# Seven-stage attention with VectorE's and ScalarE's instructions held in written order

## The chip, the cores and the metric

The kernel runs on one core of a Trainium2 chip. The metric is the device time of one execution in microseconds; the median of three runs before the change is 8564.84 us (8560.8, 8564.84 and 8583.75). A core has five engines with an instruction stream each: PE (TensorE, matrix products; PEld is its loading of weights), DVE (VectorE), ACT (ScalarE), POOL (GpSimd, here it only starts gathers) and SP (SyncE, here it starts loads and stores). They work side by side and wait for each other through semaphores.

## The reference, cut to what matters

A graph of 12500 nodes with 256 features and 200000 edges, sorted by their target node. Three neighbourhood-averaging layers come first, then an attention step over the same edges. The change touches the attention alone:

```python
x = _layernorm(x + sage(x))                          # three layers, not touched
ZU = einsum('nd,kdr->knr', Z, U)                     # 4 heads of 16
zs, zd = ZU[:, src, :], ZU[:, dst, :]
logits = (zs * zd).sum(-1) / 4
alpha = softmax of logits over the edges of one dst
agg = segment_sum(alpha[..., None] * zs, dst)        # per head and node
ssa = einsum('k,knr,kdr->nd', softmax(head_w), agg, U)
Z_half = 0.5 * Z + 0.5 * ssa
DZ = Z_half @ Dmat.T
grad_step = Z_half + 0.5 * ((Z_half - DZ @ Dmat) @ Dmat)
x = _layernorm(x + relu(grad_step - 0.05))
```

## The kernel before, in words

`fast_sage` computes the three layers, and `fast_attention` the rest. In the profiled execution attention starts at about 6106 us and runs to the end.

Attention cuts the sorted edges into 112 groups of 14 x 128 edges. A group's edges end in a window of 128 target nodes; a node whose edges run over a border is carried into the next group. For each group:

- SP loads the window's rows: `zn` (64 projected features of the targets), `zb` (the features to which the step is added), `zT` (the features turned, for the gradient), and into `ohT` the edges' target positions, spread over 128 partitions.
- POOL gathers the 14 x 128 source rows of 64 features into `zs`, 14 indirect DMAs (line 119). There are six `zs` buffers, so the gathers of group g can start only when group g-6 has read its own for the last time, in `wf` (L1002).
- DVE makes the one-hot matrix `oh` (L453) and ACT its transpose `ohT` (Abs L974, Relu L975). ACT and DVE split `zn` into a rounded part and a rest, `z2` (L979, L980).
- PE multiplies `ohT` by `z2`, 14 products in two halves (`pD`, L986): each edge's target row. There are two `pD` buffers in PSUM, one for each half.
- For each half, DVE multiplies `zs` by `pD` (`zz`, L993) and sums (`lg`, L996), ACT takes the exponential (L999) and copies it to PSUM (`pe`, L1001), DVE weights `zs` (`wf`, L1002), and ACT and DVE split it into `w` (L1005, L1006).
- PE sums `w` over the edges of each node: 14 products of `oh` and `w` and one that carries the last group's rest (`pA`, L1009, L460, with `sh` made by DVE at L459). ACT and DVE add the two parts (`part` L1016, `acc` L1018), DVE divides (`den` L384, L385, `ag` L387), PE turns the result (`pT`, L1022), ACT copies it (`agT`, L394).
- PE makes the gradient step, two products of `zT` (L376) and one of `agT` (L377) into `pO`; ACT applies the relu (L401), DVE adds `zb` (L402) and normalizes (L332, L333, sqrt on ACT L335, L336, L337); SP stores (L435).

`pA`, `pT` and `pO` have one PSUM buffer each. The exponential and the square root need different function tables on ACT, so a table load stands ahead of each once a round.

A group is a generator of five parts, and a round of the loop runs the first part of a new group and then the next part of each of the four groups before it. PE's products are chained in the order in which the program writes them (`in_order`). DVE's and ACT's instructions are not: the scheduler of the build orders them. In the built program one round's order is, on PE: pT, pA with its carry, pD, L376, L377. On ACT: z2, Exp of the first half, relu, pe, Exp, pe, w, Abs, w, sqrt, agT, Relu, part. On DVE: both wf, den's reciprocal, the addition of zb, wlo, ag, the norm's statistics, z2's rest, wlo, the norm, the one-hot, zz, acc, lg, zz, den, sh, lg.

Two helpers are needed to read the diff. `after(first, then)` holds two instructions of one engine in that order, without a semaphore. `store_rows` puts the store on SP behind the instruction that made the tile.

Of the kernel before, what the change touches and what calls it, by code (L numbers as in the profile page):

```python
# [22 lines left out]
P = 128  # L23
# [24 lines left out]
def tile_gnn_resnorm(  # L48
# [137 lines left out]
    with tc.tile_pool(name="prep", bufs=1) as prep, \  # L186
# [136 lines left out]
        nc.vector.tensor_mul(hrow, hrow, hrec)  # L323
        nc.vector.tensor_scalar(gu, ptu[:KR, :], hrow, 0.5, op0=OP.mult, op1=OP.mult)


    def layernorm(wk, y, o):

        n = y.shape[0]
        st = wk.tile([n, nc.vector.BN_STATS_DIM], F32, name="bn_st")  # L330
        mv = wk.tile([n, nc.vector.BN_AGGR_DIM], F32, name="bn_mv")
        nc.vector.bn_stats(st, y)  # L332
        nc.vector.bn_aggr(mv, st)  # L333
        rs = wk.tile([n, 1], F32, name="bn_rs")
        nc.scalar.activation(rs, mv[:, 1:2], AF.Sqrt, bias=eps_t[:n])  # L335
        nc.vector.reciprocal(rs, rs)  # L336
        return nc.vector.tensor_scalar(o, y, mv[:, 0:1], rs, op0=OP.subtract, op1=OP.mult)  # L337

    def sage_end(wk, l, wts, po, hn, xb):

# [36 lines left out]
        mm.append(nc.tensor.matmul(pg, agT, gu, start=False, stop=True))  # L377
        return pg, mm[0], mm[-1]

    def attention_mean(wk, acc, eps, op):  # L380

        n = acc.shape[0]
        den = wk.tile([n, K], F32, name="den")
        nc.vector.tensor_scalar(den, acc[:, KR:AW], eps, None, op0=op)  # L384
        nc.vector.reciprocal(den, den)  # L385
        ag = wk.tile([n, KR], F32, name="ag")
        nc.vector.tensor_mul(ag.rearrange("p (k r) -> p k r", r=R),  # L387
                             acc[:, :KR].rearrange("p (k r) -> p k r", r=R),
                             den.unsqueeze(2).to_broadcast([n, K, R]))
        return ag  # L390

    def attention_turned(wk, pt, n):
        agT = wk.tile([KR, n], F32, name="agT")
        nc.scalar.activation(agT, pt[:KR], AF.Copy)  # L394
        return agT

    def attention_end(wk, zz, pg):

        n = zz.shape[0]
        g = wk.tile([n, D], F32, name="g")  # L400
        nc.scalar.activation(g, pg, AF.Relu, bias=shrink[:n])  # L401
        nc.vector.tensor_add(g, zz, g)  # L402
        return g, layernorm(wk, g, g)

# [40 lines left out]
        nc.vector.tensor_copy(c, iota[:, :n])  # L447
        return c

    def onehot(wk, nodes, r, dt=F32, name="oh", op=OP.is_equal, bufs=2):  # L450

        oh = wk.tile([P, GT, P], dt, name=name, bufs=bufs)
        nc.vector.tensor_tensor(oh, r.unsqueeze(2).to_broadcast([P, GT, P]),  # L453
                                nodes.unsqueeze(1).to_broadcast([P, GT, P]), op=op)
        return oh

    def carry(wk, pa, d, before):
        sh = wk.tile([P, P], F32, name="sh")
        nc.vector.tensor_scalar(sh, steps, d, None, op0=OP.is_equal)  # L459
        return nc.tensor.matmul(pa, sh, before, start=False, stop=True)  # L460

    def fast_sage():
# [482 lines left out]
    def fast_attention():  # L945
        loads[0] = None
        H = GT // 2
        with tc.tile_pool(name="att", bufs=2) as wk, \
                tc.tile_pool(name="att_c", bufs=1, space=PSUM) as cps, \
                tc.tile_pool(name="att_ps", bufs=1, space=PSUM) as ps:  # L950
            nodes = group_consts(cps)
            order, sums = [None], [None]

            def in_order(first, last):
                if order[0] is not None:
# [3 lines left out]
            def group(g):  # L959

                zb = wk.tile([P, D], F32, name="zb", bufs=8)
                zT = wk.tile([P, DC, P], F32, name="zT", bufs=6)
                zn = wk.tile([P, KR], F32, name="zn", bufs=3)
                load_rows([(zn, zu_d), (zb, z_d), (zT, zt_d)], g)

                ohT = wk.tile([P, GT, P], F32R, name="ohT", bufs=3)
                rT = ohT.bitcast(F32).rearrange("p j e -> p (j e)")
                nc.sync.dma_start(rT, rel_d[g * GT:(g + 1) * GT, :].rearrange("j e -> (j e)")[None, :]
                                  .to_broadcast([P, GT * P]))
                zs = wk.tile([P, GT, KR], F32, name="zs", bufs=6)  # L970
                for j in range(GT):
                    gather(zs[:, j], zu_d, srcI[:, g, j:j + 1])
                oh = onehot(wk, nodes, rel[:, g], F32R, bufs=3)
                nc.scalar.activation(ohT.rearrange("p j e -> p (j e)"), rT, AF.Abs, bias=npidx)  # L974
                nc.scalar.activation(ohT.rearrange("p j e -> p (j e)"), rT, AF.Relu, scale=-1.0, bias=1.0)  # L975

                z2 = wk.tile([P, K, 2, R], F32R, name="z2", bufs=3)
                zk = zn.rearrange("p (k r) -> p k r", r=R)
                nc.scalar.activation(z2[:, :, 0], zk, AF.Copy)  # L979
                nc.vector.tensor_tensor(z2[:, :, 1], zk, z2.bitcast(F32)[:, :, 0], op=OP.subtract)  # L980

                w = wk.tile([P, GT, 2 * AW], F32R, name="w", bufs=3)
                for a in (0, H):

                    pd = ps.tile([P, (H + 1) * 2 * KR], F32, name="pD", bufs=2)
                    mm = [nc.tensor.matmul(pd[:, j * 2 * KR:(j + 1) * 2 * KR], ohT[:, a + j],  # L986
                                           z2.rearrange("p k i r -> p (k i r)"), start=True, stop=True)
                          for j in range(H)]
                    in_order(mm[0], mm[-1])

                    zg = zs[:, a:a + H].rearrange("p t (k r) -> p (t k) r", r=R)
                    zz = wk.tile([P, H * K, 2, R], F32, name="zz")
                    nc.vector.tensor_mul(zz, zg.unsqueeze(2).to_broadcast([P, H * K, 2, R]),  # L993
                                         pd[:, :H * 2 * KR].rearrange("p (m i r) -> p m i r", i=2, r=R))
                    lg = wk.tile([P, H, K], F32, name="lg")
                    nc.vector.reduce_sum(lg.rearrange("p t k -> p (t k)"), zz.rearrange("p m i r -> p m (i r)"),  # L996
                                         axis=AX.X)
                    wf = wk.tile([P, H, AW], F32, name="wf")
                    nc.scalar.activation(wf[:, :, KR:], lg, AF.Exp, scale=0.25)  # L999
                    pe = pd[:, H * 2 * KR:H * (2 * KR + K)].rearrange("p (t k) -> p t k", k=K)  # L1000
                    nc.scalar.activation(pe, wf[:, :, KR:], AF.Copy)  # L1001
                    nc.vector.tensor_mul(wf[:, :, :KR].rearrange("p t (k r) -> p t k r", r=R),  # L1002
                                         zs[:, a:a + H].rearrange("p t (k r) -> p t k r", r=R),
                                         pe.unsqueeze(3).to_broadcast([P, H, K, R]))
                    nc.scalar.activation(w[:, a:a + H, :AW], wf, AF.Copy)  # L1005
                    nc.vector.tensor_tensor(w[:, a:a + H, AW:], wf, w.bitcast(F32)[:, a:a + H, :AW], op=OP.subtract)  # L1006
                yield
                pa = ps.tile([P, 2 * AW], F32, name="pA")
                mm = [nc.tensor.matmul(pa, oh[:, j], w[:, j], start=j == 0, stop=g == 0 and j == GT - 1)  # L1009
                      for j in range(GT)]  # L1010
                if g:
                    mm.append(carry(wk, pa[:, :AW], delta[:, g:g + 1], sums[0]))
                in_order(mm[0], mm[-1])
                yield
                part = wk.tile([P, AW], F32, name="part")
                nc.scalar.activation(part, pa[:, AW:2 * AW], AF.Copy)  # L1016
                acc = wk.tile([P, AW], F32, name="acc", bufs=3)
                nc.vector.tensor_add(acc, part, pa[:, :AW])  # L1018
                sums[0] = acc
                ag = attention_mean(wk, acc, 1e-30, OP.max)  # L1020
                pt = ps.tile([P, P], F32, name="pT")
                mm = nc.tensor.transpose(pt[:KR], ag, ident)  # L1022
                in_order(mm, mm)
                yield
                agT = attention_turned(wk, pt, P)
                pg, *mm = gradient_step(ps, zT, agT)
                in_order(*mm)
                yield
                o, made = attention_end(wk, zb, pg)
                store_rows([(o, out)], g, made)  # L1030
                yield

            live = []
            for g in range(NG + 4):
                if g < NG:
                    live.append(group(g))
                    next(live[-1])
                old = live[:-1] if g < NG else live  # L1040
                for s in old:
                    next(s)
                if g >= 4:
                    live.pop(0)
            assert not live


    NTE = E // TE
# [104 lines left out]
    def general_attention():  # L1153
# [40 lines left out]
        with tc.tile_pool(name="go", bufs=1) as wk, tc.tile_pool(name="go_ps", bufs=1, space=PSUM) as ps:  # L1194
            with tc.For_i(0, NBLK, 1) as i:
# [7 lines left out]
                pt = ps.tile([P, NB], F32, name="pT")  # L1203
                nc.tensor.transpose(pt[:KR], attention_mean(wk, ab, 1e-16, OP.add), ident[:NB, :NB])
                pg = gradient_step(ps, zT, attention_turned(wk, pt, NB))[0]
                o, _ = attention_end(wk, zb, pg)
                nc.sync.dma_start(out[rows, :], o)

    ok = nc.values_load(flag[0:1, 0:1], min_val=0, max_val=1)
# [40 lines left out]
```

## Time and profile before

| | us |
|---|---|
| median of three runs | 8564.84 |
| profiled execution, its own time | 8592.77 |
| its span | 8591.0 |
| busy PE, PEld | 5679.5, 4428.1 |
| busy DVE | 3946.6 |
| busy ACT | 3631.0 |
| busy POOL | 4832.6 |
| attention's first gather starts | 6106.16 |
| the last round of gathers starts | 8482.39 |

Busy time is the time in which an engine worked on its own instructions; it covers the whole kernel. POOL's records are the issuing of the gathers. Since the stages have different limits, the sums over the whole span say little about attention, which is the last 29% of it. Durations of single instructions in a steady round of attention, in us: gather 0.94 (0.30 from one to the next), zz 1.08, lg 1.08, one-hot 2.02, wf 0.62, wlo 0.65, Abs 1.77, Relu 1.68, w copy 0.60, table load 1.28, relu 0.47, the norm's statistics 0.42 and its last step 0.41, addition of zb 0.39; 14 pD or 14 pA products 3.23 each. All times are from one profiled execution. The end of a matrix product in the records is worked out by the profiler, not observed; a wait that is put down to "issue" or "remote" is one for which the profile shows no releaser.

### The profile page before, as it was taken

To read this page: it belongs to the slowest core of one execution; us is meant where nothing else is said; L and a number is where in the kernel's file an instruction comes from. 1 tells how busy PE (TensorE), PEld (TensorE's weight loads), DVE (VectorE), ACT (ScalarE), POOL (GpSimd) and SP (SyncE) were. 2 spreads that over 40 slices of the span, in tenths; PEclk is the share of its full clock that TensorE was granted. 3 is DMA by queue.
4 is the path that set the end of the run, shared out by engine and by line. 5 is a ranking of instruction groups with operands and counts; after the bars stand their busy time and mean duration, and the time that the engine had idled before them with its cause. 6 is when DMAs were issued, how large, how long until landed. Compare 5 with 4: busy or idle time off the path is not lost.

```text
span 8591.0 us, 86683 instructions
## 1 busy us (share of the span) xinstructions
PE 5679.5 (66%) x23308; PEld 4428.1 (52%) x23308; DVE 3946.6 (46%) x10013; ACT 3631.0 (42%) x6727; POOL 4832.6 (56%) x5038
## 2 busy tenths in 40 slices
PE   4677777777768888887578878888334444444445
PEld 3455455556646666666466666666233333333334
DVE  4555444433433344444344545454344544444445
ACT  2444444444434444444344444444234444344444
POOL 5555555555555555555455555555456665666663
PEclk8788888888878888998789989998655555555555
DMA  7645555567656666666466666666222222223222
GB/s 208 223 159 166 164 166 183 189 210 228 213 160 199 196 211 208 212 208 200 143 187 193 196 192 205 193 198 182 77 75 85 84 84 83 83 84 86 84 83 69
DMA packets 878810, 1367.37 MB, mean 159 GB/s; under 512 B 191090, under 2 KB 533130, under 8 KB 874207
## 3 DMA queue, kind: packets, MB, share of 16 engines
q1 hardware_dynamic: 629744, 802.71, 28.9%
q0 software_dynamic: 216000, 504.16, 20.9%
q10 hardware_dynamic: 32559, 54.81, 1.8%
q8 instruction: 187, 3.06, 0.2%
q14 instruction: 320, 2.62, 0.1%
HBM read 1150.87 MB, written 210.33 MB: 158 GB/s over the span
## 4 chain that ended last, share of the span: by engine, by line
PE 18%; issue 9%; DVE 8%; another core or an unknown queue 8%; POOL 3%; DMA 2%; ACT 2%; SPq 0%; DVEq 0%; ACTq 0%; POOLq 0%
PE px L740 5%; POOL zs L119 3%; PE pA L1009 2%; PE pA L843 2%; PE pD L986 2%; DVE hl L837 1%; PE pO L376 1%; DVE zz L993 1%; DVE wf L1002 1%; PE pO L352 1%; DMA zs<-zu_d,srcI 1%; DVE lg L996 1%; PE pT L361 1%; PE pO L377 1%
## 5 line engine op out<-in xcount | busy, mean ns | idle before, releaser
L119 POOL DMA_INDIRECT xg<-h_d,srcI x2128 | 2052.9, 965 | 1614.4 <-issue 486.8
L740 PE MATMUL px<-c,hz 128*128 128x512 f32 x7840 | 2386.3, 443 | 339.2 <-issue 166.4
L119 POOL DMA_INDIRECT zs<-zu_d,srcI x1568 | 1487.0, 948 | 988.2 <-issue 456.8
L740 PEld LDWEIGHTS px<-c,hz 128*128 128x128 f32 x7840 | 1580.1, 207 | 821.6 <-issue 314.9
L119 POOL DMA_INDIRECT xg<-in_x_dram,srcI x1274 | 1230.7, 966 | 1038.3 <-PE pA L851 461.7
L734 ACT ACTIVATE c<-c 128x1024 fp32r<-128x1024 uint8 (+1 forms) x1176 | 1061.5, 913 | 1656.4 <-remote 641.7
L453 DVE TENSOR_TENSOR oh<-rel,gconst 128x1792 fp32r<-128x1792 f32 (+1 forms) x358 | 722.7, 2019 | 935.4 <-remote 594.6
L837 DVE TENSOR_TENSOR hl<-xg,hl 128x256 fp32r<-128x256 f32 x2128 | 783.3, 420 | 594.5 <-ACT hl L835 427.7
L1022 PE MATMUL pT<-ident,ag 128*64 128x128 f32 x112 | 47.1, 421 | 1334.6 <-DVE ag L387 1181.3
L633 ACT ACTIVATE win<-pc 128x392 uint8<-128x392 f32 x1024 | 477.9, 500 | 700.3 <-remote 287.5
L1022 PEld LDWEIGHTS pT<-ident,ag 128*64 128x64 f32 x112 | 14.4, 128 | 1417.0 <-DVE ag L387 1255.2
L835 ACT ACTIVATE hl<-xg 128x512 fp32r<-128x512 f32 x1216 | 620.3, 567 | 261.4 <-PE pA L843 72.6
L843 PE MATMUL pA<-hl,oh 128*128 128x512 f32 x2128 | 612.0, 424 | 49.0 <-issue 46.4
L630 PE MATMUL pc<-ob,oa 128*128 128x392 bf16 x1024 | 343.9, 361 | 400.7 <-issue 175.6
L843 PEld LDWEIGHTS pA<-hl,oh 128*128 128x128 f32 x2128 | 427.7, 204 | 157.8 <-issue 52.7
L851 PE MATMUL pA<-xg,oh 128*128 128x258 f32 x1764 | 467.1, 412 | 10.8 <-ACT agg L886 8.2
L352 PE MATMUL pO<-ws,hT 128*128 128x256 f32 x984 | 321.5, 457 | 157.0 <-DVE zu L371 58.9
L851 PEld LDWEIGHTS pA<-xg,oh 128*128 128x128 f32 x1764 | 363.7, 210 | 107.1 <-issue 35.4
L352 PEld LDWEIGHTS pO<-ws,hT 128*128 128x128 f32 x984 | 214.3, 226 | 367.8 <-issue 165.6
L986 PE MATMUL pD<-z,ohT 128*128 128x128 f32 x1568 | 362.0, 418 | 57.9 <-issue 32.2
L363 DVE COPY hT<-pT 128x512 f32<-128x512 f32 x246 | 168.8, 686 | 475.8 <-remote 136.6
L1002 DVE TENSOR_TENSOR wf<-zs,pD 128x448 f32<-128x448 f32 x224 | 130.5, 618 | 557.5 <-issue 493.9
(251 smaller groups left out, 8559.6 us busy)
## 6 DMA issues: line engine op xcount, KB each, us to landing
hz<-hs_d SPq DMA_DIRECT2D x588, 512.0 KB
c<-cnt_d SPq DMA_DIRECT2D x112, 896.0 KB
ohT<-rel_d SPq DMA_DIRECT2D x112, 896.0 KB
hs_d<-hs SPq DMA_DIRECT2D x218, 256.0 KB
cnt_d<-win ACTq DMA_DIRECT2D x32, 1568.0 KB
xg<-h_d,srcI POOLq DMA_INDIRECT x2128
c<-cnt_d SPq DMA_DIRECT2D x56, 448.0 KB
zs<-zu_d,srcI POOLq DMA_INDIRECT x1568
```

Source lines behind the costliest of these rows:

```text
L119: return nc.gpsimd.indirect_dma_start(out=dst_ap, out_offset=None, in_=table, in_offset=bass.IndirectOffsetOnAxis(ap=idx, axis=0))
L352: mm = [nc.tensor.matmul(po, hT[:, i], wts[i // DC][:, i % DC], start=i == 0, stop=i == 2 * DC - 1) for i in range(2 * DC)]
L453: nc.vector.tensor_tensor(oh, r.unsqueeze(2).to_broadcast([P, GT, P]), nodes.unsqueeze(1).to_broadcast([P, GT, P]), op=op)
L630: mm = nc.tensor.matmul(pc.rearrange("p b d -> p (b d)"), oa[:, c], ob[:, c], start=True, stop=True)
L633: nc.scalar.activation(win[:, :, d:d + NC], pc, AF.Copy)
L734: nc.scalar.activation(c32.rearrange("p (k d) -> p k d", d=P), c8[:, :, b % CB], AF.Copy)
L740: made.append(nc.tensor.matmul(px[f][i], hz[:, b % ZB, a:a + P].bitcast(F32R), c32[:, i * 512:(i + 1) * 512], start=b == 0 and part == 0, ...
L835: nc.scalar.activation(hi[:, b + j:b + j + n, :W], xg[:, a + j:a + j + n, :W], AF.Copy)
L837: nc.vector.tensor_tensor(lo[:, b + j, :D], xg[:, a + j, :D], hf[:, b + j, :D], op=OP.subtract)
L843: mm.append(nc.tensor.matmul(pa, oh[:, a + j], hl[:, j].rearrange("p i d -> p (i d)"), start=first, stop=stop))
L851: mm.append(nc.tensor.matmul(pa[:, :W], oh[:, a + j], xg[:, a + j, :W], start=first, stop=stop))
L986: mm = [nc.tensor.matmul(pd[:, j * 2 * KR:(j + 1) * 2 * KR], ohT[:, a + j], z2.rearrange("p k i r -> p (k i r)"), start=True, stop=True) f ...
```

## The change

The group becomes a generator of seven stages (numbered 0 to 6 below), and a round g visits them in the order of a written list, with each stage at a group of its own age. `Line` is a wrapper around an engine that chains every instruction made through it behind the one before. All DVE and ACT instructions of attention go through it, so that their order on the engine is the order in which the round's stages are written. The attention's end is cut into `attention_step` (relu, addition), `row_stats` (statistics, sqrt) and `normed` (reciprocal, last step). `zT` gets seven buffers instead of six and `oh` four instead of three; `zs` keeps six.

```diff
+    class Line:
+        def __init__(self, engine):
+            self.engine, self.last = engine, None
+        def __getattr__(self, name):
+            def call(*args, **kwargs):
+                i = getattr(self.engine, name)(*args, **kwargs)
+                if self.last is not None:
+                    after(self.last, i)
+                self.last = i
+                return i
+            return call
...
+            ve, ac = Line(nc.vector), Line(nc.scalar)
...
-                zT = wk.tile([P, DC, P], F32, name="zT", bufs=6)
+                zT = wk.tile([P, DC, P], F32, name="zT", bufs=7)
...
                     gather(zs[:, j], zu_d, srcI[:, g, j:j + 1])
-                oh = onehot(wk, nodes, rel[:, g], F32R, bufs=3)
+                yield
+                oh = onehot(wk, nodes, rel[:, g], F32R, bufs=4, ve=ve)
...
                     in_order(mm[0], mm[-1])
+                    halves.append((a, pd))
+                yield
+                w = wk.tile([P, GT, 2 * AW], F32R, name="w", bufs=3)
+                weights = []
+                for a, pd in halves:
...
+                    weights.append((a, wf, pe))
+                for a, wf, pe in weights:
+                    ve.tensor_mul(wf ...)
+                    ac.activation(w[:, a:a + H, :AW], wf, AF.Copy)
+                for a, wf, pe in weights:
+                    ve.tensor_tensor(w[:, a:a + H, AW:], ...)
                 yield
...
-                o, made = attention_end(wk, zb, pg)
+                o = attention_step(wk, zb, pg, ve, ac)
+                yield
+                stats = row_stats(wk, o, ve, ac)
+                yield
+                made = normed(o, o, *stats, ve)
                 store_rows([(o, out)], g, made)
                 yield
...
-            live = []
-            for g in range(NG + 4):
-                if g < NG:
-                    live.append(group(g))
-                    next(live[-1])
-                old = live[:-1] if g < NG else live
-                for s in old:
-                    next(s)
-                if g >= 4:
-                    live.pop(0)
-            assert not live
+            groups, stages = [group(g) for g in range(NG)], (0, 6, 5, 4, 6, 3, 2, 6, 1)
+            for g in range(NG + max(stages)):
+                for stage in stages:
+                    if 0 <= g - stage < NG:
+                        next(groups[g - stage])
```

In the list a number is the age of the group that is advanced: 0 is loads and gathers of group g; the first 6 the relu and addition of g-6; 5 agT and the gradient's products of g-5; 4 part, acc, the division and pT of g-4; the second 6 the norm's statistics and sqrt of g-6; 3 pA with its carry and sh of g-3; 2 everything from zz to wlo of g-2; the last 6 the norm's end and the store of g-6; 1 the one-hots, z2 and pD of g-1. The built program has this order on every engine. On PE: L376, L377, pT, pA with its carry, pD. On ACT: relu, agT, part, sqrt, Exp, pe, Exp, pe, w, w, Abs, Relu, z2. On DVE: addition of zb, acc, den, its reciprocal, ag, statistics, sh, zz, lg, zz, lg, wf, wf, wlo, wlo, the norm's two last steps, the one-hot, z2's rest. The order of the gathers on POOL is as before, and so is everything ahead of attention.

## The prediction

> **What bounds the kernel now.** I read first the view of windows. Its columns are the stretch, its length, busy us (and instructions) of PE, PEld, DVE, ACT and POOL, the granted clock, the DMA share and GB/s. The rows are the start of attention, its steady part, and its end after the last gather:
>
> ```profile
> 6106.00:6246.00 140.00, 12.96 (x56) 12.24 (x56) 25.15 (x32) 22.89 (x30) 106.00 (x112) 0.50 0.27 73
> 6289.00:8482.00 2193.00, 987.50 (x3774) 829.16 (x3774) 1071.80 (x2042) 905.30 (x1530) 1354.22 (x1428) 0.50 0.30 84
> 8500.00:8568.00 68.00, 49.98 (x194) 42.30 (x194) 51.84 (x102) 38.48 (x74) 0.00 (x0) 0.50 0.14 48
> ```
>
> The steady part holds 1428 gathers, which is 102 rounds of 14: 2193/102 = 21.5 us a round. Per round PE is busy 9.7, DVE 10.5, ACT 8.9 and POOL 13.3 us, plus 0.30 us between gathers, 17.4 in all. Nobody fills 21.5. Next I read one such round in the timeline (start, length, engine, line, operation; in brackets the idle time before and who ended it):
>
> ```profile
> 6330.45 0.95 POOL L119 DMA_INDIRECT zs<-zu_d,srcI  x1 [3.26 <-DVE den L385]
> ...
> 6334.83 3.23 PE L986 MATMUL pD<-z,ohT 128*128 128x128 f32 x14
> ...
> 6339.80 1.22 PE L377 MATMUL pO<-gu,agT 64*128 64x256 f32 x2
> 6340.34 1.09 DVE L993 TENSOR_TENSOR zz<-zs,pD 128x896 f32<-128x896 f32 x1 [1.50 <-PE pO L376]
> ...
> 6345.97 0.57 SPq L430 DMA_DIRECT2D zT<-zt_d  x1
> 6346.75 0.94 POOL L119 DMA_INDIRECT zs<-zu_d,srcI  x1 [0.30 <-issue]
> ...
> 6348.95 0.47 ACT L401 ACTIVATE g<-pO,shrink 128x256 f32<-128x256 f32 x1 [6.81 <-issue]
> ...
> 6349.54 1.15 DVE L1002 TENSOR_TENSOR wf<-zs,pD 128x448 f32<-128x448 f32 x2 [6.85 <-issue]
> ...
> 6350.96 0.94 POOL L119 DMA_INDIRECT zs<-zu_d,srcI  x1 [3.27 <-DVE den L385]
> ```
>
> POOL's next round starts 0.27 us after the second wf (L1002) ends at 6350.69: six zs buffers, so gathers of g wait for wf of g-6. ACT reaches the second Exp and pe only behind the relu (L401), and the relu starts 7.9 us after its product (L377) is recorded as done (6341.02). Without gathers the same step is:
>
> ```profile
> 8505.14 0.42 PE L1022 MATMUL pT<-ident,ag 128*64 128x128 f32 x1 [12.19 <-DVE ag L387]
> ...
> 8513.60 1.22 PE L377 MATMUL pO<-gu,agT 64*128 64x256 f32 x2
> ...
> 8514.86 0.47 ACT L401 ACTIVATE g<-pO,shrink 128x256 f32<-128x256 f32 x1 [1.17 <-PE pO L377]
> ...
> 8517.76 0.42 PE L1022 MATMUL pT<-ident,ag 128*64 128x128 f32 x1 [2.94 <-DVE ag L387]
> ```
>
> There the relu starts 0.04 us after the product, and a round takes 12.6 us (8517.76 - 8505.14). So what I must price is lateness: while POOL gathers, TensorE's ends reach the others late. The waiters of the long start, 112 gathers in a row from 6106.16, give the rate:
>
> ```profile
> 6166.26 1.09 DVE L993 TENSOR_TENSOR zz<-zs,pD 128x896 f32<-128x896 f32 x1 [14.84 <-remote]
> 6205.47 0.23 ACT L1016 ACTIVATE part<-pA 128x68 f32<-128x68 f32 x1 [36.07 <-remote]
> 6225.06 1.09 DVE L993 TENSOR_TENSOR zz<-zs,pD 128x896 f32<-128x896 f32 x1 [16.61 <-remote]
> 6244.66 1.09 DVE L993 TENSOR_TENSOR zz<-zs,pD 128x896 f32<-128x896 f32 x1 [18.51 <-remote]
> ```
>
> They wait for 14 pA, 7 pD and 7 pD products in turn: steps of 39.2, 19.6 and 19.6 us, 2.80 us a product. In the steady round the 30th, 32nd and 33rd product after POOL's start are noticed at 9.9 (zz), 15.5 (zT's load) and 18.5 us (relu): 2.8 to 3.0 each. The first 23 (up to the first zz at 6336.62, placed as without gathers) are on time. When POOL pauses, the backlog clears:
>
> ```profile
> 8148.54 0.94 POOL L119 DMA_INDIRECT zs<-zu_d,srcI  x1 [0.30 <-issue]
> ...
> 8154.14 0.23 ACT L1016 ACTIVATE part<-pA 128x68 f32<-128x68 f32 x1 [20.86 <-remote]
> ...
> 8161.91 0.94 POOL L119 DMA_INDIRECT zs<-zu_d,srcI  x1 [12.43 <-DVE den L385]
> ```
>
> Here two rounds of gathers ran on end; 4.7 us after their end (8149.48) everything late arrives at once, and POOL restarts 12.4 us after its end.
>
> On the Trainium skill, Perfetto Trace Analysis, the part on the Tensor Engine instruction: TensorE's end is computed from the instruction's size, and the push of its semaphore is not profiled. The rows above agree (an end at 6341.02, its waiter at 6348.95); by recorded ends alone the sum would be the 17.4 us round of the last rival.
>
> **The change part by part.** Its starting point is 8591.0 us of span, 8592.8 profiled, 28 (0.33%) above the median of 8564.84, so I scale by 0.9967 at the end. Everything ahead of attention (to 6106) is the same program: 0. Instructions per round are the same in number and shape: 0. Neither zT's seventh buffer nor oh's fourth moves the gathers, bound to zs's six: 0. SP's queue, order store, zn, zb, zT, ohT: zT waits for L376 of g-7, ohT for the products of g-3, and all loads are asked for a round ahead of use; cover is one round, at least 12 us against landings of 0.3 to 1.4; uncovered, 1.4 a round.
>
> **The new round, POOL's restart (0.26 behind the second wf) at 0.** Behind it ACT has w copy 0.60, Abs 1.77, Relu 1.68, z2 0.26: 4.3; DVE the wlo, rs, normed, one-hot 2.02: less. z2lo 0.21 ends about 4.4 with a handover, and pD's 14 products (3.23) run from 4.4 to 7.6. Then the round behind: relu .47, agT .25, part .21 on ACT, then acc .22, den .17, rec .17, ag .22, stats .42, aggr .18, sh .28 on DVE, so the first zz starts at 7.0. From there zz 1.08, lg 1.08, zz 1.08, lg 1.08, wf 2 x 0.62 = 5.5: **second wf at 12.4**. The two table loads (1.28 each) end at 8.1, before the first lg at 9.1: hidden; uncovered, 1.28. Without lateness a round is thus 12.5, as the 12.6 now.
>
> Lateness: the start-up line is post(n) = 5.5 + 2.8(n - 8) behind POOL's start; with the products run in the first 5.5 us counted as free ((5.5 - 4.4)/0.23, about 5), pD's 14th comes at 5.5 + 2.8 x 1 = 8.3, before the second zz asks for it at 9.2. All the rest that this round waits for (relu, agT, part) came before POOL's restart. So the relu no longer stands before wf, and its 5.3 us a round ((345.5 + 199.5)/102, the waits ended by "remote" and "issue" ahead of L401) go from here.
>
> What is late next: wf at 12.4 lies before the gathers' end at 17.4, so POOL gets leave early and runs 28 gathers on end, to 34.8. The products of that second round come at 13.9 (L376), 16.7 (L377), 19.5 (pT), then 14 pA and a carry, which at 2.8 would come at 61.5. Its reader, part (L1016), now stands in the chain before all of the round's zz, and acc before every DVE instruction after it. They wait for the clearing: 34.8 + 4.7 = 39.5; part to sh 2.3, zz to wf 5.5: 47.3, restart at **47.5**. That is the row above: restart 12.4 behind the gathers' end there, 12.7 here. Two rounds cost 47.5, 23.75 each, against 21.5.
>
> Bounds for the pair: least if the buffer counts 26 products from POOL's restart, as the steady round read alone would allow (pA's end then comes during the second run, pair 43.8 to 45.3); most if pD's second half is late by 2 more: 49.5. The start-up run speaks for the small buffer, so I take 47.5.
>
> Sum: 51 pairs x (47.5 - 43.0) = +229; start-up +2; the tail behind the last batch's start, now 108.6 (8591.0 - 8482.4), I estimate at 98 (batch 17.4, clearing 4.7 and 7.8, three full rounds of 12.5, five emptier ones): -10. **+221**: 8814 profiled, x 0.9967 = **8785**.
>
> The clock is 0.50 in all three windows; I keep it. The Trainium skill, TensorE: Matmul & The Clock Gate, Part 1, has the gate release after some 3.4 us of sustained work. The row decides: 9.7 us of products a round left it at 0.50. If the new order released it, that rule would halve the products' time, and the sum would be unchanged, for POOL's runs and clearings set the pair.
>
> **The rivals.**
>
> *The large buffer.* The pair costs 43.8 to 45.3: 51 x 0.8 to 51 x 2.3 less 8 = +33 to +109, 8597 to 8673; at 43.5 or less it is no change. For: 23 products on time in the steady round. Against: the start's line.
>
> *A pause in every round.* If pD is noticed at 14 to 17 instead of 7.6, the second wf (3.4 behind the second zz's start) falls at 17.4 to 20.5, POOL pauses 3 us each round, the backlog clears and none is carried over: 20.5 a round, -1.0 x 102 - 8: 8483 profiled, 8455. For: 3.3 us pauses clear it now. Against: pD comes right behind the restart.
>
> *Each round blocked (slower still).* If pD's second half is not noticed before the gathers' end, each round is 17.4 + 3.3 clearing + 4.3 = 25.0: +3.5 x 102 = +357, 8950 profiled, 8920. It decides once fewer than 14 products pass behind the restart. Against: 23 do now.
>
> *The chain does what it says and lateness goes.* Bound by POOL: 17.4 a round, -4.1 x 102 - 8 = -426: 8167 profiled, 8140. For: wf is ready at 12.4. Against: the start, where gathers alone, with little else running, gave 2.8 us a product.
>
> **How the numbers follow.** Pairs of 46 to 49.5: 0.45, 8710 to 8890. Large buffer: 0.17, of which no change 0.07. Each round blocked 0.10. Pause in every round 0.17. Bound by POOL 0.11. Slower by over 0.3% (about what a measurement here can tell from none; above 8591): 0.45 + 0.10 + 0.10 = 0.65; within: 0.07; faster: 0.28. The time is that of the pairs. The range leaves out POOL's bound and the blocked rounds: 8440 to 8890; the pairs' own range is 8710 to 8890.
>
> **What would show it.** Runs of 28 gathers with 12 to 13 us of idle POOL between; part (L1016's place) starting 4 to 5 us behind each run's end, with the largest wait on ACT; relu on time; zz 7 us behind POOL's restart in the first round of a pair. Wrong: POOL without pauses (bound by POOL), a pause of 3 us in each round (8455), or part on time in the second run (large buffer).

## The result and the profile after

The changed kernel took 8804.88 us (median of 4 runs, 8783.66 to 8850.55), against 8574.3 us for the kernel before (median of 4, 8560.8 to 8616.86): a ratio of 1.0267, with a 95% interval of 1.0212 to 1.0323. The prediction was 8785, 1.026 of the time before.

The windows of the changed kernel, cut at the start of its first run of 28 gathers and at the start of its last batch (columns as in the prediction):

```profile
6338.00:8750.00 2412.00, 1034.42 (x3774) 839.89 (x3774) 1145.37 (x2039) 940.42 (x1531) 1378.38 (x1429) 0.50 0.27 77
8767.00:8848.00 81.00, 62.01 (x221) 49.14 (x220) 61.52 (x127) 47.29 (x86) 0.38 (x1) 0.50 0.14 46
```

The same 102 rounds of gathers that took 2193 us now take 2412: 23.65 us a round instead of 21.5. Every engine is busy for only 2 to 7% longer than before (PE 1034 against 987, DVE 1145 against 1072, ACT 940 against 905, POOL 1378 against 1354 us), and none fills the round, so the 219 us are waiting. The clock is 0.50 as before.

The waits of the changed kernel from 6200 to 8800 us (engine, tile, line, who ended the wait: us in total, times, longest). All that goes through the wrapper is recorded under its line, 334, so the tile's name tells which instruction it is:

```profile
DVE acc L334 <- ACT part L334: 1057.3, 52, 29.7
ACT part L334 <- remote: 1016.6, 52, 29.5
...
POOL zs L119 <- DVE wf L334: 637.1, 52, 23.2
```

The same view of the kernel before, from 6200 to 8500 us:

```profile
POOL zs L119 <- DVE den L385: 405.6, 86, 12.4
ACT g L401 <- remote: 345.5, 54, 8.2
...
ACT g L401 <- issue: 199.5, 31, 7.5
```

Before, POOL waited 86 times for 405.6 us, and ACT waited for relu's product (`g`) in most rounds. Now relu is no longer among the long waits, POOL waits 52 times, and each time for about 12 us; ACT's part waits as often, about 20 us each. One pair of rounds in the timeline of the changed kernel shows why there are 52 and not 102:

```profile
7329.93 1.25 POOL L119 DMA_INDIRECT zs<-zu_d,srcI  x1 [12.07 <-DVE wf L334]
...
7336.24 1.09 DVE L334 TENSOR_TENSOR zz<-zs,pD 128x896 f32<-128x896 f32 x1
...
7340.64 1.22 DVE L334 TENSOR_TENSOR wf<-zs,pD 128x448 f32<-128x448 f32 x2
...
7343.48 0.63 PE L482 MATMUL pA<-acc,sh 128*128 128x68 f32 x2
...
7349.13 0.47 ACT L334 ACTIVATE g<-pO,shrink 128x256 f32<-128x256 f32 x1 [3.08 <-issue]
...
7364.29 0.94 POOL L119 DMA_INDIRECT zs<-zu_d,srcI  x1 [0.30 <-issue]
...
7369.67 0.23 ACT L334 ACTIVATE part<-pA 128x68 f32<-128x68 f32 x1 [18.85 <-remote]
...
7371.57 1.09 DVE L334 TENSOR_TENSOR zz<-zs,pD 128x896 f32<-128x896 f32 x1
...
7375.81 1.23 DVE L334 TENSOR_TENSOR wf<-zs,pD 128x448 f32<-128x448 f32 x2
...
7377.31 1.25 POOL L119 DMA_INDIRECT zs<-zu_d,srcI  x1 [12.08 <-DVE wf L334]
```

(The last POOL line is the next pair's first.) The second wf ends 11.9 us behind POOL's restart, while POOL still has four gathers of the batch to start, and 28 gathers run on end. The carry (L482) is recorded as done at 7344.11, but its reader, part, starts at 7369.67, 4.4 us after POOL has stopped (7365.23). From there it takes 7.4 us to the end of the wf that lets POOL go on, and 7.6 to POOL's restart. In the whole of attention 51 such runs of 28 gathers follow each other, 47.3 us from one start to the next, against 98 single batches and 3 double ones before.

### The profile page after: what moved, and what is told of

Its sections match the earlier page's. It is cut to its first block, busy times and chain, and to the rows that moved or that the text cites. A ratio compares the mean times of both kernels' runs of the same rounds, so it can differ in the third digit from the quotient of the medians.

```text
span 8848.8 us, 87008 instructions
## 1 busy us (share of the span) xinstructions
PE 5738.9 (65%) x23308; PEld 4450.9 (50%) x23308; DVE 4028.5 (46%) x10013; ACT 3667.5 (41%) x6727; POOL 4857.0 (55%) x5038
## 3 DMA queue, kind: packets, MB, share of 16 engines
q0 software_dynamic: 216000, 504.16, 20.5%
## 5 line engine op out<-in xcount | busy, mean ns | idle before, releaser
L119 POOL DMA_INDIRECT zs<-zu_d,srcI x1568 | 1511.9, 964 | 1189.2 <-DVE wf L334 637.1
L475 DVE TENSOR_TENSOR oh<-rel,gconst 128x1792 fp32r<-128x1792 f32 (+1 forms) x246 | 496.5, 2018 | 708.7 <-remote 344.5
L1009 PEld LDWEIGHTS pD<-z,ohT 128*128 128x128 f32 x1568 | 342.9, 330 | 632.2 <-issue 588.9
L334 DVE TENSOR_TENSOR acc<-part,pA 128x68 f32<-128x68 f32 x112 | 24.8, 222 | 1111.5 <-ACT part L334 1060.9
L334 ACT ACTIVATE part<-pA 128x68 f32<-128x68 f32 x112 | 24.6, 219 | 1052.8 <-remote 1016.6
```

Source lines behind the costliest of these rows:

```text
L119: return nc.gpsimd.indirect_dma_start(out=dst_ap, out_offset=None, in_=table, in_offset=bass.IndirectOffsetOnAxis(ap=idx, axis=0))
L334: i = getattr(self.engine, name)(*args, **kwargs)
L475: ve.tensor_tensor(oh, r.unsqueeze(2).to_broadcast([P, GT, P]), nodes.unsqueeze(1).to_broadcast([P, GT, P]), op=op)
```

## The experiments

The runs fell on several chips, and two kinds of chip showed. On one kind the kernel before takes 6,617 to 6,638 us (chips 8, 10 and 11), on the other 8,560 to 8,711 (chips 1 and 12, and the first measurements of both kernels, whose chip is not on record). I call them prompt and late. Each of these chips was used at one time only, so the runs don't tell whether a chip is always of its kind or was in that state at the time. Each ratio below is to the kernel before on the same chip, with its 95% interval. The expectations of the first four runs (the gathers taken out, half of them, the order not held, the pause) were written before a prompt chip had been seen; all four ran on one, and their times, which are those of a late chip, missed.

**The gathers taken out**, on a prompt chip and, as load_b, on a late one:

```diff
-                for j in range(GT):
-                    gather(zs[:, j], zu_d, srcI[:, g, j:j + 1])
+                nc.sync.dma_start(zs, zu_d[:GT * P, :].rearrange("(j p) c -> p j c", p=P))
```

> The changed kernel with POOL's 14 gathers of a group replaced by one load that SP starts: the same number of rows of 64 features, but always the table's first 1792 rows instead of the edges' sources. Theory (TensorE's ends reach the others late while POOL gathers, and the changed order loses by that alone): relu follows L377 and part follows the carry within 0.1 us, rounds of 12.5 to 13 us, attention about 118 x 12.6 = 1490 us instead of 2695, time about 7,560 to 7,650. Rival (the held order is slow in itself, its instructions wait in a chain whatever POOL does): part still waits tens of us in every second round, and rounds stay above 20 us, time above 8,400. Second rival (small rows as such make TensorE late, whoever starts the transfer): as the first rival in time.

> The changed kernel with the gathers of attention replaced by one load a group that SP starts (the table's first 1792 rows instead of the edges' sources), once more, on whatever chip this call gets. Theory: where the kernel before takes 8,570 to 8,690 (TensorE late under gathers), the three layers keep their time to about 6,100, and in attention nothing is late any more: rounds of 12 us, attention about 1,380 us instead of 2,695, time about 7,500. Where it takes about 6,630: 6,000 again. Rival (that chip's TensorE is late whatever POOL does): part stays late, rounds above 20, time above 8,400 on the first kind of chip.

Measured: 5998.76 us, ratio 0.905 (0.9032 to 0.9068), on the prompt chip; 7502.88, ratio 0.8708 (0.8654 to 0.8762), on the late one, where about 7,500 was expected. Attention alone (from its first instruction to the end) takes 1368.2 us on the first and 1367.7 on the second. A stretch of load_b, windows and timeline:

```profile
6200.00:7450.00 1250.00, 1032.40 (x3880) 859.48 (x3879) 1157.74 (x2099) 950.58 (x1573) 0.00 (x0) 0.50 0.50 149
```

```profile
6904.65 0.63 PE L482 MATMUL pA<-acc,sh 128*128 128x68 f32 x2
...
6907.37 0.21 ACT L334 ACTIVATE part<-pA 128x68 f32<-128x68 f32 x1
```

The carry ends at 6905.28, and part starts without any idle time in front of it (no bracket), behind agT on its engine. Rounds are 11.9 us: the held order by itself is no slower than the 12.6 that the old one needs without gathers. So the 230 us are not the chain's own, and they are not those of small rows as such: the same number of rows of the same size arrives, on a late chip too. They go with the gathers that POOL starts. The first rival falls, and so does the second. The edit changes three things at once, though: who starts the transfer, the queue that it goes through (software_dynamic in the profile for the gathers, hardware_dynamic for SP's loads), and the rows themselves (the table's first 1792 instead of scattered ones). Which of them matters is not shown.

**Half of the gathers**, on a prompt chip:

```diff
-                for j in range(GT):
+                for j in range(H):
                     gather(zs[:, j], zu_d, srcI[:, g, j:j + 1])
+                nc.sync.dma_start(zs[:, H:], zu_d[:H * P, :].rearrange("(j p) c -> p j c", p=P))
```

> The changed kernel with 7 gathers a group; the other 7 tiles of 128 rows come by one load that SP starts, of the table's first 896 rows instead of the edges' sources. Theory: POOL is done 8.7 us behind its start, before the second wf at 12.0; the pause of 3 to 4 us clears the lateness (about 1.9 + 0.1 x 7 = 2.6 us behind the last gather), no runs of two batches, rounds of 12.5 to 14 us, time about 7,560 to 7,750. Rival (lateness grows with the number of products whatever the gathers' number): rounds near 23 us, time near 8,800.

Measured: 6003.6 us, ratio 0.9057 (0.9039 to 0.9075), 12.05 us a round. Since nothing is late on this chip, it says only that gathers stop being the bound at half their number; how the lateness grows with them was not tried on a late chip.

**Both kernels once more**, on a prompt chip:

> The changed kernel itself, unedited, on the chip of this call. Theory as put in the prediction (TensorE's ends come late under gathers and the changed order turns that into runs of 28 gathers): if this chip shows the lateness at all, 1.02 to 1.03 of the time before and runs of 28 with 12 us between; if it doesn't, as in the run without chaining (rounds of 17.7 us, POOL without a pause), before and after are both bound by the gathers, and the ratio is 0.99 to 1.01. Rival (the held order costs 230 us by itself, on any chip): 1.02 or more here too, with part or acc waiting.

> The kernel before, unedited, for a trace of it on the chip of this call. Theory: where its time is near 6,630, the relu follows L377 within 0.1 us and POOL gathers without a pause, 17.4 to 17.7 us a round; where it is near 8,570, relu is 7 to 8 us late and rounds are 21.5. Rival (the time of 6,630 comes from the three layers alone): attention takes 2,480 us here as well.

Measured: 6634.97 us for the changed kernel, a ratio of 1.0015 (1.0006 to 1.0025); 6629.05 for the kernel before. Attention takes 2012.3 and 2003.1 us. In the kernel before on this chip:

```profile
5505.23 1.22 PE L377 MATMUL pO<-gu,agT 64*128 64x256 f32 x2
...
5506.48 0.47 ACT L401 ACTIVATE g<-pO,shrink 128x256 f32<-128x256 f32 x1 [1.17 <-PE pO L377]
...
5509.65 1.09 DVE L993 TENSOR_TENSOR zz<-zs,pD 128x896 f32<-128x896 f32 x1 [5.38 <-DMA zs<-zu_d,srcI]
```

Its windows, and those of the changed kernel on the same chip:

```profile
4700.00:6580.00 1880.00, 1033.00 (x3955) 868.62 (x3956) 1124.81 (x2135) 951.38 (x1594) 1425.83 (x1491) 0.50 0.36 102
```

```profile
4700.00:6580.00 1880.00, 1045.09 (x3929) 870.63 (x3929) 1194.16 (x2127) 962.39 (x1595) 1427.23 (x1486) 0.50 0.36 102
```

The relu starts 0.03 us behind its product although POOL gathers, where on the late chip it was 7.9 us. What a zz waits for is the landing of its own gathered rows. Both kernels start some 1,490 gathers in the 1,880 us, one each 1.26 us, without a pause: rounds of 17.65 and 17.72 us. There the new order has nothing to gain (all waits but the gathers' are hidden already) and next to nothing to lose. The rival by which the order costs 230 us on any chip falls; so does the one that put the difference between the chips into the three layers alone, although these differ as well: attention starts at 4,620 to 4,631 us on prompt chips and at 6,106 to 6,235 on late ones.

**The order not held**, on a prompt and a late chip:

```diff
-            ve, ac = Line(nc.vector), Line(nc.scalar)
+            ve, ac = nc.vector, nc.scalar
```

> The changed kernel without the chaining of VectorE and ScalarE: same stages, same order on TensorE, the build orders the other two. In the built program part stands behind the w copies and before Relu and z2 on ACT, wf stands behind relu, and all 33 products of a round come behind POOL's restart, pD's last. Theory: the second zz waits for the 33rd product, 18.5 us behind the restart, wf comes at about 21.9, POOL pauses over 4 us in each round, no runs of 28; 22.1 us a round, 0.6 x 102 = 60 us more than before: about 8,630 (8,540 to 8,720). Rival (the stages themselves, not their chaining, cost the 230 us): about 8,800 and runs of 28. Second rival (the chaining alone costs): at or below the time before, 8,570.

> The changed kernel without the chaining of VectorE and ScalarE, once more, on whatever chip this call gets. Theory, on a chip where TensorE is late: all 33 products come behind POOL's restart, the second zz waits for pD's last, 18.5 us behind the restart or the clearing at 20.6; wf at 22 to 24; runs of 14, 1.005 to 1.03 of the time before. On the other kind of chip: the time before, within 0.3%. Rival (the stages alone make runs of 28 and 1.027): runs of 28 here too. Second rival (the chaining alone costs): 1.00 or less.

Measured: on the prompt chip 6623.78, a ratio of 0.9994 (0.9984 to 1.0004); on the late one 8734.37, 1.0137 (1.0075 to 1.0199). The second is within the expected ratios, but not for the expected reason. There are 51 runs of 28 gathers, as in the full change, and none of the expected single batches:

```profile
7135.97 3.23 PE L1041 MATMUL pA<-w,oh 128*128 128x136 f32 x14
...
7139.20 0.95 POOL L119 DMA_INDIRECT zs<-zu_d,srcI  x1 [10.12 <-DVE sh L481]
...
7147.88 1.15 DVE L1033 TENSOR_TENSOR wf<-zs,pD 128x448 f32<-128x448 f32 x2
...
7170.89 2.02 DVE L475 TENSOR_TENSOR oh<-rel,gconst 128x1792 fp32r<-128x1792 f32 x1 [21.43 <-remote]
...
7172.98 1.32 POOL L119 DMA_INDIRECT zs<-zu_d,srcI  x1 [0.31 <-issue]
...
7176.49 0.23 ACT L1048 ACTIVATE part<-pA 128x68 f32<-128x68 f32 x1 [25.68 <-remote]
```

I had put all of a round's products behind POOL's restart. But pA's 14 run before it, at 7135.97, and with them out of the way the next wf ends at 7149.03, 9.8 us behind the restart and well within the batch. So the stages alone bring the runs of 28, as the first rival had it; holding the order costs the rest. Attention takes 2621.8 us here, 2695.8 in the full change and 2485.1 before, so by these three executions (the first on chip 12, the others from the first measurements) some 137 of the 211 us come from the stages and 74 from the order. The one-hot at 7170.89 needs the end of the second round's pA, the 32nd product behind the restart in the order of the program, and gets it 31.7 us behind it, 3.4 us before POOL stops: products are noticed one by one while POOL gathers, not only when it pauses. Over the 51 pairs of this execution the one-hot's wait ends 12.2 to 33.8 us behind the restart, 27.5 in the median, and in 34 of the pairs (the one shown is not among them) even part starts before POOL stops. In the full change part starts behind POOL's stop in every one of the 51 pairs, 39.7 us behind the restart in the median.

**A pause behind each batch** (`rest` has 128 x 1200 elements, `pool` holds POOL's instructions in order), on a prompt and a late chip:

```diff
-                    gather(zs[:, j], zu_d, srcI[:, g, j:j + 1])
+                    pool.append(gather(zs[:, j], zu_d, srcI[:, g, j:j + 1]))
+                for _ in range(3):
+                    pool.append(nc.gpsimd.memset(rest, 0.0))
+                for a, b in zip(pool, pool[1:]):
+                    after(a, b)
...
```

> The changed kernel with three memsets of 1200 elements on POOL behind each group's 14 gathers, about 3 us in which POOL gathers nothing. Theory: each batch is followed by a pause, TensorE's ends clear in it, and part is no longer late by a whole batch: runs of 14, 17.4 + 3.1 to 3.4 = 20.5 to 20.9 us a round, against 21.5 before and 23.65 after: about 8,480 to 8,520, faster than both kernels although POOL has more to do. Rival (the order on VectorE and ScalarE costs the time, POOL's runs follow from it): no gain, 8,800 or more, up to 112 x 3 = 340 more.

> The changed kernel with the three memsets behind each group's gathers once more, on whatever chip this call gets. Theory: where the kernel before takes about 8,570 (TensorE's ends late under gathers), the pause of 3.6 us clears the lateness in each round: runs of 14, 20.9 us a round, about 8,500, less than before. Where it takes about 6,630, nothing is late and the pause is simply added: 20.9 instead of 17.7 a round, about 6,980. Rival (the held order costs the time): near 8,800 or above on the first kind of chip.

Measured: on the prompt chip 6984.14, a ratio of 1.0533 (1.0515 to 1.055): the pause is simply added, 20.90 us a round. On the late one 8586.79, against 8688.2 for the kernel before: 0.9879 (0.9805 to 0.9953).

```profile
7005.56 0.94 POOL L119 DMA_INDIRECT zs<-zu_d,srcI  x1 [0.30 <-issue]
7006.51 3.42 POOL L998 MEMSET rest<- 128x1200 f32 x3
7009.72 1.09 DVE L334 TENSOR_TENSOR zz<-zs,pD 128x896 f32<-128x896 f32 x1 [7.58 <-DMA zs<-zu_d,srcI]
7010.09 0.95 POOL L119 DMA_INDIRECT zs<-zu_d,srcI  x1 [0.15 <-issue]
...
7017.68 0.21 ACT L334 ACTIVATE part<-pA 128x68 f32<-128x68 f32 x1
```

POOL pauses 3.58 us behind each 14 gathers, part starts without idle time in front of it, and a round takes 20.96 us, nearly the same as on the prompt chip. The last wait of a round is the second zz's, and it mostly ends in the pause: 2.0 us (median) behind the last gather's end, where it is 1.6 on the prompt chip. POOL has three instructions more in every round, and yet the kernel is 1.2% faster than the kernel before on this chip (two executions against three), where the change without the pause was 2.7% slower on the first one. Attention takes 2370.7 us, against 2485.1 before and 2695.8 in the full change in the first measurements, and 2363.5 with the pause on the prompt chip. This is the strongest support for the theory: what the change lost was the pause in which TensorE's late ends come through. It is no improvement for all chips, since it costs 5.3% on a prompt one.

**zz ahead of part**, on a late chip:

```diff
-            groups, stages = [group(g) for g in range(NG)], (0, 6, 5, 4, 6, 3, 2, 6, 1)
+            groups, stages = [group(g) for g in range(NG)], (0, 6, 5, 6, 2, 4, 3, 6, 1)
```

> The changed kernel with the stages in the order 0, 6, 5, 6, 2, 4, 3, 6, 1: everything from zz to wlo now stands ahead of part, acc and pT, so that wf no longer waits for the carry. Theory: on a chip where TensorE is late, all of pT, pA, carry and pD come behind POOL's restart, pD's second half is noticed only when POOL pauses, runs of 14, about 24.3 us a round: near 8,870. On a chip where it isn't, POOL's gathers bound both: 17.6 us a round, the time before within 0.5%. Rival (part ahead of zz is what costs, and without it wf is free): below the time before on the first kind of chip.

Measured: 8828.32 against 8688.2, 1.0157 (1.0106 to 1.0209), 22.8 us a round. Both theories missed the pattern. There are 56 single batches and 24 double ones, with pauses of 1.3 to 3.5 us in front of some and of 9 to 11 us in front of most; pD is noticed in some rounds within the batch (15 to 17 us behind the restart) and in others only with the clearing. My 24.3 us took the second case for all rounds. That it isn't faster than before shows that taking part out of wf's way doesn't free wf: the next late product, pD, holds it.

**Fewer products, and a later leave for POOL**, both on a prompt chip:

```diff
                 mm = [nc.tensor.matmul(pa, oh[:, j], w[:, j], start=j == 0, stop=g == 0 and j == GT - 1)
-                      for j in range(GT)]
+                      for j in (0, GT - 1)]
```

> The changed kernel with 2 of pA's 14 products (the first and the last tile of edges; the sums of the other 12 are left out). Theory (lateness goes by the number of products, 2.8 us each, while POOL gathers): on a chip where TensorE is late, the carry is the 21st product behind POOL's restart instead of the 33rd; L377, the 17th, was noticed 19.2 us behind the restart in the changed kernel, so part now starts at about 19.2 + 4 x 2.8 = 30 us, within the second batch, instead of at 39.5; the next products in line, pD of the round, still come only with the clearing, so zz waits until 39.5 in part's place, wf at 45, a pair of 45 instead of 47.3, 22.6 a round, about 1.014 of the time before. Rival (part is held by the clearing alone, whatever the number of products): part at 39.5, pair 47.3, 1.027. On a chip where TensorE isn't late: the time before within 0.5%.

```diff
...
+                    if g >= 5:
+                        tc.add_manual_dep(i.ins, second[g - 5].ins.name, DONE, reason="gathers behind the products")
```

(in the second kernel, for each gather `i`; `second` holds the second zz of each group)

> The changed kernel with each group's gathers waiting, besides its buffer, for the second zz of the group five before, which moves POOL's leave from behind wf to the zz 8.6 us behind it. Theory, on a chip where TensorE is late: now 31 products follow the restart up to pD's end; by the steady round of before (30th noticed at 9.9, 32nd at 15.5) the last is noticed at about 12.7, still before the gathers' end at 17.4: runs of 28 as before this edit; part waits for the clearing at 39.5, the second zz comes at 44.0, a pair of 44.2, 22.1 a round, about 1.007 of the time before. Rival (one batch a round as soon as more products follow the restart): runs of 14 with a pause of 3 us, 20.7 a round, 0.99. On the other kind of chip: no wait decides but the gathers, the time before within 0.5%.

Measured: ratios of 1.0012 (1.0001 to 1.0024) and 1.0017 (1.0006 to 1.0029). Neither landed on a late chip, so neither tells its theories apart; on a prompt one both are bound by the gathers, as expected for it. Whether the number of products sets the lateness is therefore not shown by any run on a late chip.

## Why the prediction was right, point by point

The prediction gave the mechanism and, by the profiled executions, each of its terms:

| step of the prediction | predicted | measured |
|---|---|---|
| first zz behind POOL's restart | 7.0 | 6.3 (7336.24 - 7329.93) |
| second wf's end, first round | 12.4 | 11.9 |
| relu of the second round (L377) | 16.7 | 19.2 (7349.13) |
| part of the second round, by the clearing | 39.5 | 39.7 (7369.67) |
| next restart: the pair | 47.5 | 47.4; 47.3 over all 51 pairs |
| 51 pairs against 102 rounds before | +229 | +219 (2412 - 2193) |
| start-up | +2 | +1 |
| tail behind the last batch's start | -10 | -10 (98.9 against 108.6) |
| attention in all | +221 | +211 (2695.8 - 2485.1) |

The two profiled spans differ by more, 257.8 us. The other 47 lie ahead of attention, which starts at 6153.0 instead of 6105.9, in code that is the same in both programs. Late chips scatter by as much on the kernel before (8,561 to 8,711 us), and I know of no cause for that part. The ratio of the medians holds what attention alone gives: 1 + 211/8591 = 1.0245, in the interval.

**What bounds the kernel.** Right, for the chip of the profile: lateness of TensorE's ends under gathers. With the gathers gone it is gone (load_b), with pauses between the batches it costs nothing more (pause_b). What the profile of before could not show is that this depends on the chip, or on its state at the time. On a prompt chip both kernels are in the state that the prediction called bound by POOL, 17.7 us a round, and the change does nothing that matters. Nothing in the prediction provided for that: it was luck that the changed kernel, too, was timed where TensorE's ends come late; on chip 10 the ratio is 1.0015.

**The relu's wait, and what is late next.** Right. The 5.3 us a round ahead of relu went from wf's way, POOL got its leave at 11.9 us, and the carry's reader took the wait's place.

**The small buffer.** The prediction chose the start-up line over the steady round's 26 products. The choice was right in its effect, since part came with the clearing; the size was off for the relu, 19.2 instead of 16.7. Had none of the products counted as free, the line would give 5.5 + 2.8 x 9 = 30.7, so about four products, (30.7 - 19.2)/2.8, did for the five assumed. The line is a rough measure, though, and its 2.80 us no constant. The prediction took the 2.8 to 3.0 us a product of the steady round as the same rate, but the start's pA and pD products are one record each in the trace, while L376's two products are four records and L377's one is two: counted by records the steady round needs 1.4 to 1.5 us each, half of the start's 2.80. For the 32nd product in the kernel without chaining, counting the 16 that run in the first 5.5 us as free, the line gives 5.5 + 2.8 x 8 = 27.9, and the median is 27.5, but single pairs lie between 12.2 and 33.8. For pD's last in the kernel with zz first, the 30th with 16 free, it gives 5.5 + 2.8 x 6 = 22.3, where 15 to 17 was seen. Why part is held until the clearing in all pairs of the full change, and in only 17 of the 51 without chaining, is not shown.

**The held order.** The prediction weighed the order as a whole and did not ask what part of it makes the runs. The run without chaining shows that the stages do, by putting pA ahead of wf.

**The rivals.** A pause in every round is what pause_b makes by force, at 20.96 us a round for the 20.5 worked out. Rounds blocked one by one did not happen in the changed kernel; a pD noticed only with the clearing was seen in part of the rounds of the kernel with zz first.

**What stays open.** What makes a chip late, and whether it is always so; whether the number of products alone sets the lateness (the run that was to tell fell on a prompt chip); how it grows with the number of gathers in a batch; and what in the gathers makes it, the issuing, the queue or the scattered rows. Since TensorE's recorded ends are computed, the records don't tell either whether its products end late or are only reported late. No version was found that beats both kernels on both kinds of chip.

## What to carry to other kernels

Before an engine is made to finish earlier, ask what its finishing starts, and whether somebody lived on the gap: here POOL's 3 us of waiting were the time in which others caught up. Where a wait moves from one tile to another, look at the queue behind the new waiter: part stood in front of all of VectorE's round. And when a profile shows an effect that nothing in the program explains, run the kernel before on another chip, or at another time, before tuning to it.

## What the runs showed of the hardware that was not expected

The same program takes 6,617 to 6,638 us on three chips and 8,560 to 8,711 on others. While POOL's gathers run on a late chip, TensorE's ends reach the others late, in the start at 2.80 us a product. Later in a run of gathers TensorE's own products start further apart, too: in the second batch of the changed kernel's pair its records stand 1.4 to 2.8 us apart, at 0.6 us each. That many products are outstanding then may be the reason, but no run tested it:

```profile
7353.34 0.58 PE L398 MATMUL pO<-gz,zT 128*128 128x256 f32 x1 [1.50 <-issue]
...
7355.57 0.59 PE L398 MATMUL pO<-gz,zT 128*128 128x256 f32 x1 [1.66 <-issue]
...
7357.68 0.58 PE L399 MATMUL pO<-gu,agT 64*128 64x256 f32 x1 [1.51 <-issue]
...
7360.48 0.58 PE L399 MATMUL pO<-gu,agT 64*128 64x256 f32 x1 [2.22 <-issue]
```

The gathers themselves are no slower there (0.94 us and 0.30 between them on both kinds). ScalarE's signals are not late: in the second half of the pair's first batch VectorE's part of z2 starts 0.03 us behind ScalarE's (7346.09 behind 7346.06). VectorE's are not either: the second Exp starts 0.04 us behind lg (7340.76 behind 7340.72). Memsets on POOL do not hold the late ends up (the second zz starts 2.0 us, in the median, behind the last gather's end, within the memsets' 3.4), and loads of as many rows that SP starts do not make them late (attention 1367.7 us on a late chip, 1368.2 on a prompt one).

The two kinds differ ahead of attention as well: there the granted clock is 0.86 to 0.87 in the six executions on late chips and 0.95 to 0.96 in the eight on prompt ones, while in attention it is 0.50 in all fourteen. Whether the lower clock has to do with the lateness, or only follows from TensorE's longer waits there, is not shown.
